# A Mamba block and a ternary FFN on one core: four steps cut into pieces, and every piece placed anew

## The chip, the cores and the metric

One core of a Trainium2 chip. The metric is the device time of one execution in microseconds, the median of several runs; lower is better. Engines: PE (matrix), DVE (vector), ACT (scalar functions and table lookups), POOL (GpSimd), and SP, whose queue issues most of the DMAs.

## The reference

Input x is 2 x 4096 x 256, all float32. Two residual layers follow each other:

```python
x = x + layernorm(mamba(layernorm(x)))      # W_in 1024x256, W_out 256x512
x = x + layernorm(ffn(layernorm(x)))        # hidden 1024, ternary weights

# mamba, per token t, 512 channels e, 16 states s
x_path, z = split(x @ W_in.T); x_path = silu(x_path)
B, C, dt_in, lam_in = split(x_path @ W_x.T)       # 16, 16, 1, 1
B, C = rope(rmsnorm(B + bias)), rope(rmsnorm(C + bias))   # angle: cumulative mean of dt
dt = softplus(dt_in * W_dt + b_dt);  lam = sigmoid(lam_in)
dA = exp(A * dt)
u  = (1 - lam) * dt * dA * Bx_prev + lam * dt * Bx        # Bx = B * x_path
h  = dA * h + u;  y = sum_s(h * C)                        # the scan over t
y  = (y + x_path * D) * silu(z);  out = y @ W_out.T

# ffn
h = gelu(layernorm(x) @ tern(w1).T + b1);  out = layernorm(h) @ tern(w2).T + b2
```

## The kernel before

The sequence is cut into 16 blocks of 512 tokens, 8 for each batch element; the scan state is carried from block to block. A block's scan is cut into 64 units: 4 channel parts j of 128 channels, in each 4 state rounds q of 4 states, in each 4 columns c. A unit is a tile of 128 rows (32 channels x 4 states) by 512 tokens. Four units of one (j, q) make a group and share a tile g.

For one group the work goes round like this:
- `inputs` (L1076): POOL multiplies B by the loaded weighted input `vr` into g, 128 x 2044.
- `decay` (L232): ACT computes exp(A dt) of one unit into a PSUM bank `da`; there are four such banks. `enter` (L1084) writes the carried state into the first column of g.
- `unit_scan`: DVE runs the recurrence. For the first `SPLIT[q]` columns (2, 1, 2, 1 for the four rounds) the result stays in `da` (L1092), and DVE multiplies it by C (`product_v`, L1115, and a copy of the last state, L1116); for the other columns it goes into g (L1095).
- `last` (L1104): ACT copies the last states out of g. `product_g` (L1111): POOL multiplies those columns of g by C in place.
- `sum` (L1127): PE sums the states of the whole g into the bank `y`. Then g is free; there are three g buffers. `start_y` (L1121) has put the skip term `dx` into `y` before, `gate` (L1139) multiplies the finished `y` by silu(z). There is one `y` bank.

Beside the scan of block k run two plans. The plan ahead prepares block k + 1: norm, projections (`project`, `keep`), silu of x, the B/C projection (`bc_project`), softplus of dt (`softplus`), transposes of dt (`dt_turn`, `dt_keep`), the diagonal matrices `mix` and `ddot` (`diag_lam`, `diag_dot`, L912), with which PE weights dt (`weigh`, `skip`, L927), silu of z (`silu_z`), angles, sines and rotations, stores of dt, v and B/C to DRAM and their loads in scan layout (`load_dt`, `load_v`, `load_b`, `load_c`, by SP). `initial` (POOL, `ini`) makes the carried state. The plan behind takes block k - 1 through the output projection, the residual, the norm, the first FFN layer (`ffn_1`, `ffn_keep`), Gelu, the second layer (`ffn_2`, L1202 and L1211, then `ffn_sums`, `ffn_out`), the last norm and the store (`finish`, L1263). Block 0's preparation has a table of places of its own, and in block 0 a plan of 29 steps (`W_AT`) prepares the ternary weights.

The order is written out by hand. A unit has three places; a block has 192. Each step of the plans has a place in `AT` (in `AT_FIRST` for block 0), each step of the scan a distance `LAG` from its unit:

```python
due.setdefault(max(3 * u + lags[i], 0), []).append((what, u))
...
at_place(3 * base)
at_place(3 * base + 1)
if cur is not None:
    unit_scan(cur, j, q, c)
at_place(3 * base + 2)
```

A place is only an order: each engine takes its instructions in the order in which they were issued and waits for what each one needs. Where a tile has no free buffer yet, its instruction stands behind the one that frees it. ACT loads a function table whenever `special` (L230, L232) asks for a function that the loaded table lacks: Exp and Ln share one, Silu and Sin another, Softplus and Gelu have their own.

Of the kernel before, what the change touches and what calls it, by code (L numbers as in the profile page):

```python
# [8 lines left out]
F32 = mybir.dt.float32  # L9
# [5 lines left out]
P = 128  # L15
# [34 lines left out]
    "decay": (-4, -6, -5, -7, 1, -1, 0, 1, -2, -2, -4, -11, 0, -8, -8, -9, 1, 1, -2, -4, -2, -1, -3, -8, -5, -5, -3, -3, 1, -7, -2, -13, -5, -4, -6, -3, -3, -3, -3, -2, -5, -7, 0, -2, -11, -9, -8, -3, -3, -4, -8, -12, -8, -4, -2, -3, -5, -7, -3, -7, -2, 0, -11, -11,),  # L50
    "inputs": (-7, -4, -1, -5, -5, -7, -1, -13, -4, -11, -5, -1, -8, -4, -4, 0,),
    "enter": (-5, -7, -9, -4, -9, -6, -7, -8, -5, -5, -8, -7, -9, -9, -8, -1,),
    "product_v": (8, 20, 4, 4, 7, 4, 4, 4, 5, 9, 4, 4, 11, 4, 4, 4, 11, 10, 4, 4, 4, 4, 4, 4, 7, 4, 4, 4, 4, 4, 4, 4, 23, 6, 4, 4, 5, 4, 4, 4, 5, 2, 4, 4, 5, 4, 4, 4, 3, 11, 4, 4, 2, 4, 4, 4, 5, 4, 4, 4, 11, 4, 4, 4,),
    "last": (21, 12, 11, 11, 12, 15, 14, 14, 19, 12, 11, 8, 16, 12, 20, 11,),
    "product_g": (30, 18, 14, 15, 13, 23, 16, 14, 24, 13, 16, 22, 22, 17, 20, 11,),
    "gate": (26, 31, 37, 25,),
    "start": (24, 17, 19, 27,),
    "sum": (31, 25, 19, 22, 20, 28, 17, 26, 24, 20, 19, 25, 38, 21, 28, 17,),
}

W_AT = (4, 20, 54, 57, 59, 63, 64, 76, 72, 62, 90, 103, 73, 77, 103, 115, 127, 152, 153, 156, 157, 144, 160, 167, 169, 169, 174, 175, 183)
AT = {
    "a_stats": (8, 9,),
    "a_power": (15,),
    "a_offset": (16,),
    "a_apply": (16, 16,),
    "a_turn": (19, 19,),
    "a_evict": (20, 20,),
    "project": (23, 30, 32, 22, 54, 62, 44, 62,),
    "keep": (25, 30, 34, 22, 62, 66, 54, 69,),  # L70
    "silu_x": (36,),
    "bc_project": (45, 48,),
    "bc_take": (61,),
    "dt_project": (75,),
    "bc_square": (98,),
    "bc_power": (112,),
    "dt_row": (75,),
    "dt_spread": (85,),
    "softplus": (89,),
    "bc_scale": (134,),  # L80
    "dt_turn": (103, 112, 110, 109,),
    "dt_keep": (106, 114, 111, 110,),
    "dt_sum": (115,),
    "angles": (125, 126, 127, 129, 130, 130, 132,),
    "diag_lam": (122,),
    "silu_z": (153,),
    "sines": (150,),
    "rotate_a": (155,),
    "rotate_b": (156,),
    "bc_turn": (159,),  # L90
    "bc_store": (163,),
    "dot_sum": (159,),
    "dot_shift": (179,),
    "dot_take": (180,),
    "weigh": (122, 132, 147, 161,),
    "weigh_x": (130, 132, 157, 169,),
    "over": (132,),
    "over_x": (134,),
    "spread": (171,),
    "carry": (177,),  # L100
    "diag_dot": (192,),
    "skip": (206, 201, 198, 195,),
    "skip_x": (208, 205, 206, 197,),
    "initial": (181, 226,),
    "x_next": (190,),
    "load_dt": (137, 217, 246, 278,),
    "load_v": (138, 234, 236, 322,),
    "load_b": (183, 170, 198, 218,),
    "load_c": (185, 186, 192, 212,),
    "x_load": (27,),  # L110
    "out_project": (39, 41,),
    "out_square": (39, 49,),
    "out_power": (39, 52,),
    "residual": (47, 54,),
    "h_stats": (52, 58,),
    "h_power": (61,),
    "h_offset": (63,),
    "h_apply": (68, 63,),
    "h_turn": (68, 71,),
    "h_evict": (74, 76,),  # L120
    "ffn_1": (82, 95, 83, 112, 94, 88, 116, 104,),
    "ffn_keep": (83, 101, 85, 119, 98, 94, 124, 109,),
    "gelu": (128, 129,),
    "ffn_2": (137, 150, 165, 184,),
    "ffn_sums": (144, 158, 175, 196,),
    "ffn_out": (148, 162, 180, 199,),
    "ffn_square": (170, 172, 199, 200,),
    "ffn_power": (172, 206,),
    "ffn_scale": (190, 207,),
    "finish": (207, 209,),  # L130
# [3 lines left out]
    "a_stats": (-181, -241,),  # L134
    "a_power": (-177,),
    "a_offset": (-169,),
    "a_apply": (-160, -134,),
    "a_turn": (-99, -85,),
    "a_evict": (-98, -81,),
    "project": (-79, -79, -79, -79, 4, 5, 1, 5,),  # L140
    "keep": (-79, -79, -79, -79, 7, 11, 6, 15,),
    "silu_x": (-74,),
    "bc_project": (-70, -70,),
    "bc_take": (-79,),
    "dt_project": (-79,),
    "bc_square": (-79,),
    "bc_power": (-46,),
    "dt_row": (-79,),
    "dt_spread": (-79,),
    "softplus": (-79,),  # L150
    "bc_scale": (-43,),
    "dt_sum": (-53,),
    "dt_turn": (-72, -76, -79, -79,),
    "dt_keep": (-54, -56, -79, -75,),
    "angles": (-45, -43, -42, -36, -36, -33, -32,),
    "diag_lam": (-46,),
    "silu_z": (43,),
    "sines": (-32,),
    "rotate_a": (-29,),
    "rotate_b": (-29,),  # L160
    "bc_turn": (-12,),
    "bc_store": (-12,),
    "dot_sum": (-21,),
    "dot_shift": (0,),
    "dot_take": (0,),
    "weigh": (-25, 0, 13, 0,),
    "weigh_x": (-22, 0, 16, 0,),
    "diag_dot": (0,),
    "skip": (0, 0, 0, 0,),
    "skip_x": (0, 0, 1, 1,),  # L170
    "load_dt": (-70, 19, 46, 98,),
    "load_v": (-22, 40, 41, 81,),
    "load_b": (-5, -3, 0, 30,),
    "load_c": (-2, -4, 10, 43,),
    "bc_project_first": (-79, -79, -79, -79,),
    "decay_rates": (-13,),
# [4 lines left out]
def mamba_ffn_kernel(  # L181
# [574 lines left out]
    def softplus(s):  # L756
        if s.k == 0:
            special(freqs, freqs, AF.Softplus)

            nc.vector.tensor_scalar_mul(freqs, freqs, 1.0 / DI)  # L760
        s.dt = p1.tile([P, NJ, T], F32, tag="dt", name=f"dt_{s.k}")
        for j in range(NJ):
            dt = s.dt[:, j, :]
            special(dt, s.pb, AF.Softplus, scale=wdt[:, j : j + 1], bias=bdt[:, j : j + 1])
            nc.sync.dma_start(s.dt_d[j * P : (j + 1) * P, :], dt)
# [142 lines left out]
    def diagonal(s, col, name):  # L908
        t = p1.tile([P, NC4, P + 1], F32, tag="dg", name=f"{name}_{s.k}", bufs=2)
        m = mixed if name == "mix" else ident  # L910
        for c in range(NC4):
            nc.scalar.activation(t[:, c, 0 : m.shape[1]], m, AF.Copy, scale=col[:, c : c + 1])  # L912
        return t

    def diag_lam(s):
        s.mix = diagonal(s, s.lam, "mix")

    def diag_dot(s):
        s.ddot = diagonal(s, s.remdot, "ddot")
# [276 lines left out]
    def ffn_2(s, c, po=None):  # L1196

        if po is None:
            po = ps_ff.tile([P, DM + 1 + P], F32, tag="ff", name=f"pf_{s.k}_{c}")
        for f in range(NH):  # L1200
            gT = s.h1[:, f, c * P : (c + 1) * P]
            nc.tensor.matmul(  # L1202
                po[:, 0 : DM + 1],
                lhsT=gT,
                rhs=w2q[:, f, :],
                start=(f == 0),
                stop=(f == NH - 1),
                skip_group_check=True,
            )

            nc.tensor.matmul(  # L1211
                po[:, DM + 1 :],
                lhsT=gT,
                rhs=gT,
                start=False,
                stop=False,
                skip_group_check=True,
            )
        nc.tensor.matmul(
            po[:, DM + 1 :], lhsT=ident, rhs=deps, start=False, stop=True, skip_group_check=True  # L1220
        )
        s.ff["po", c] = po

    def ffn_sums(s, c):
        k, po = s.k, s.ff["po", c]
        junk = p1.tile([P, DM], F32, tag="junk", name=f"junk2_{k}_{c}")
        ss = small.tile([P, 1], F32, tag="ssf", name=f"ssf_{k}_{c}")
        nc.vector.scalar_tensor_tensor(
            junk[:, 0:P], po[:, DM + 1 :], 1.0 / HID, ident, ALU.mult, ALU.mult, accum_out=ss
        )  # L1230
        m = small.tile([P, 1], F32, tag="mf", name=f"mf_{k}_{c}")
        nc.scalar.activation(m, po[:, DM : DM + 1], AF.Square, scale=1.0 / HID)
        s.ff["rs", c] = small.tile([P, 1], F32, tag="rsf", name=f"rsf_{k}_{c}")
        root(s.ff["rs", c], m, -1.0, ss)
# [54 lines left out]
    def tail(s):  # L1289
# [42 lines left out]
        for c in range(NC4):  # L1332
            ffn_2(s, c, ps_da.tile([P, DM + 1 + P], F32, tag="da", name=f"pf_{k}_{c}"))
        rg = small.tile([P, NC4], F32, tag="rs", name=f"rg_{k}")
        so = small.tile([P, NC4], F32, tag="hsum", name=f"so_{k}")
        for c in range(NC4):
            ffn_sums(s, c)
            ffn_out(s, c)
# [27 lines left out]
    def plan_ahead(s, prev):  # L1366
# [37 lines left out]
        add("softplus", softplus, s)  # L1404
# [7 lines left out]
        add("diag_lam", diag_lam, s)  # L1412
        add("silu_z", silu_z, s, range(NJ))
# [18 lines left out]
        add("diag_dot", diag_dot, s)  # L1432
# [13 lines left out]
    def plan_behind(s):  # L1446
# [32 lines left out]
        for c in range(NC4):  # L1479
            add("ffn_2", ffn_2, s, c, i=c)  # L1480
            add("ffn_sums", ffn_sums, s, c, i=c)
            add("ffn_out", ffn_out, s, c, i=c)
# [148 lines left out]
```

## Time and profile before

| what | us |
|---|---|
| median of three runs | 1990.8 (1989.3 to 1993.0) |
| profiled execution | 1991.1 |
| its span | 1989.4 |
| busy: PE / DVE / ACT / POOL | 1787.7 / 1693.5 / 1658.7 / 1726.1 |
| one I product (L1076, 2044 wide) | 3.81 |
| one P product (L1111, 1024 or 1536 wide) | 2.00 or 2.91 |
| one scan (L1092, L1095) | 1.22, 1.21 |
| one decay (L232, 512 wide) | 0.68 |
| one table load | 1.28 |

The span is the time from the first to the last instruction in the profile. An engine's idle time is given in front of the instruction that ended it, with the engine or DMA that it had waited for. The profile models the ends of matmuls, so PE's busy time is an upper figure.

### The profile page before, as it was taken

How to read it: one execution, taken by the hardware profiler on the slowest of the kernel's cores; microseconds unless marked ns; L12 is line 12 of the kernel's file. 1: busy time of each engine (PE TensorE's matmuls, PEld its weight loads, DVE VectorE, ACT ScalarE, POOL GpSimd, SP SyncE). 2: the span in 40 equal slices, each digit the busy share in tenths (PEclk: the TensorE clock that was granted, in tenths of full speed). 3: DMA queues.
4: the chain of work that ended last, by engine and by line, in shares of the span. 5: the costliest groups of instructions: out<-in, count | busy, mean ns of one | idle time of the engine just before them, and what ended most of it. 6: DMA issues, size and time to landing. Idle time of an engine off the chain costs nothing. (4 is left out here: it accounts for less than half of the span.)

```text
span 1989.4 us, 28676 instructions
## 1 busy us (share of the span) xinstructions
PE 1787.7 (90%) x8938; PEld 1073.7 (54%) x8938; DVE 1693.5 (85%) x2742; ACT 1658.7 (83%) x3832; POOL 1726.1 (87%) x863
## 2 busy tenths in 40 slices
PE   6876998989899998999999898999989999998678
PEld 3434465554646556464655646465564646555257
DVE  1699899988979998898989889799988989898961
ACT  6666988979889897989889798898979898896754
POOL 3689999999989999999989899899999999899960
PEclk7876999999989999999989999899999999898798
DMA  6734545453454645346454534545453464545300
GB/s 118 175 90 111 134 113 138 122 142 89 124 135 114 138 118 146 88 120 152 103 138 122 142 90 123 134 116 138 118 145 89 120 152 103 138 112 139 69 22 11
DMA packets 155721, 233.41 MB, mean 117 GB/s; under 512 B 30160, under 2 KB 55824, under 8 KB 155568
## 3 DMA queue, kind: packets, MB, share of 16 engines
q1 hardware_dynamic: 153440, 230.80, 47.5%
q0 software_dynamic: 544, 0.71, 0.3%
q8 instruction: 70, 1.15, 0.3%
q14 instruction: 83, 0.68, 0.1%
q10 hardware_dynamic: 1584, 0.07, 0.1%
HBM read 188.51 MB, written 42.99 MB: 116 GB/s over the span
## 5 line engine op out<-in xcount | busy, mean ns | idle before, releaser
L1076 POOL TENSOR_TENSOR g<-b,vr 128x2044 f32<-128x2044 f32 (+1 forms) x256 | 975.2, 3812 | 113.3 <-PE y L1127 81.2
L1095 DVE TENSOR_TENSOR_SCAN g<-da,g 128x512 f32<-128x512 f32 x640 | 753.3, 1207 | 17.2 <-ACT da L232 12.0
L232 ACT ACTIVATE da<-dtr,aneg 128x512 f32<-128x512 f32 x1024 | 682.1, 683 | 64.4 <-DVE g L1095 47.2
L1111 POOL TENSOR_TENSOR g<-c,g 128x1024 f32<-128x1024 f32 (+1 forms) x256 | 626.4, 2456 | 47.7 <-ACT hl L1104 26.5
L1092 DVE TENSOR_TENSOR_SCAN da<-da,g 128x512 f32<-128x512 f32 x384 | 462.2, 1221 | 118.9 <-POOL g L1076 86.6
L1127 PE MATMUL y<-g,fold 128*32 128x512 f32 x2048 | 324.6, 650 | 44.9 <-POOL g L1111 28.9
L1202 PE MATMUL pf<-w2q,h 128*128 128x257 f32 x1024 | 312.8, 387 | 16.2 <-DVE o L1239 13.1
L651 PE MATMUL pz<-oT_a,wi 128*128 128x512 f32 x512 | 277.1, 685 | 2.0 <-ACT oT_a L603 0.7
L1180 PE MATMUL ph<-oT_h,w1q 128*128 128x512 f32 x480 | 238.2, 620 | 32.8 <-ACT h L1190 10.0
L1115 DVE TENSOR_TENSOR g<-da,c 128x512 f32<-128x512 f32 x384 | 257.3, 675 | 5.6 <-DMA c<-bc_d 3.4
L1211 PEld LDWEIGHTS pf<-h 128*128 128x128 f32 x1024 | 195.3, 191 | 27.6
L1211 PE MATMUL pf<-h 128*128 128x128 f32 x1024 | 197.2, 274 | 0.0
L651 PEld LDWEIGHTS pz<-oT_a,wi 128*128 128x128 f32 x512 | 104.7, 219 | 153.6 <-issue 101.5
L1202 PEld LDWEIGHTS pf<-w2q,h 128*128 128x128 f32 x1024 | 156.0, 192 | 33.3 <-ACT g L1084 19.8
L1180 PEld LDWEIGHTS ph<-oT_h,w1q 128*128 128x128 f32 x480 | 82.4, 191 | 153.2 <-issue 59.9
L1127 PEld LDWEIGHTS y<-g,fold 128*32 128x32 f32 x2048 | 50.0, 111 | 194.0 <-issue 60.9
L230 ACT ACT_TABLE_LOAD x97 | 124.5, 1283 | 1.7
L927 PE MATMUL pw<-ddot,dtT 128*128 128x128 f32 (+1 forms) x512 | 77.6, 296 | 49.3 <-DVE dx L1007 22.9
L1149 PE MATMUL po<-wo,zs 128*128 128x256 f32 x480 | 107.6, 382 | 0.0
L927 PEld LDWEIGHTS pw<-ddot,dtT 128*128 128x128 f32 x512 | 65.8, 193 | 69.8 <-ACT ddot L912 30.8
L1149 PEld LDWEIGHTS po<-wo,zs 128*128 128x128 f32 x480 | 90.0, 190 | 24.2 <-ACT hl L1104 11.7
L927 PEld LDWEIGHTS ps<-mix,dtT 128*128 128x128 f32 x512 | 69.4, 196 | 32.6 <-issue 30.9
(238 smaller groups left out, 2421.4 us busy)
## 6 DMA issues: line engine op xcount, KB each, us to landing
dtr<-dt_d SPq DMA_DIRECT2D x256, 256.0 KB, 5.1
vr<-v_d SPq DMA_DIRECT2D x256, 256.0 KB, 6.6
dt_d<-dt SPq DMA_DIRECT2D x64, 256.0 KB, 5.4
v_d<-v SPq DMA_DIRECT2D x64, 256.0 KB, 2.0
b<-bc_d SPq DMA_DIRECT2D x256, 64.0 KB, 2.2
c<-bc_d SPq DMA_DIRECT2D x256, 64.0 KB, 2.1
xpre<-in_L_attn_x_dram SPq DMA_DIRECT2D x16, 512.0 KB, 3.8
xpost<-in_L_attn_x_dram SPq DMA_DIRECT2D x15, 512.0 KB, 6.1
```

What stands on the lines that cost most here:

```text
L232: nc.scalar.activation(dst, src, f, **kw)
L651: nc.tensor.matmul(s.pz[e], lhsT=wi[:, kk, e * P : (e + 1) * P], rhs=s.na.oT[:, kk, :], start=(kk == 0), stop=(kk == 1),)
L927: nc.tensor.matmul(ps[:, c * P - 1 + skip : c * P - 1 + n], lhsT=s.dtT[c][:, j * P : (j + 1) * P], rhs=diag[:, c, skip:], start=start and ...
L1076: nc.gpsimd.tensor_mul(states(s, j, q)[:, :, t0:], s.bcq[0, q][:, None, t0:].to_broadcast([P, NG, T - t0]), s.ch[j, "vr"][:, :, t0:],)
L1092: nc.vector.tensor_tensor_scan(da, da, g, 0.0, ALU.mult, ALU.add)
L1095: nc.vector.tensor_tensor_scan(g, da, g, 0.0, ALU.mult, ALU.add)
L1111: nc.gpsimd.tensor_mul(g, s.bcq[1, q][:, None, :].to_broadcast([P, NG - n, T]), g)
L1115: nc.vector.tensor_mul(s.g[j, q][:, c, :], da, s.bcq[1, q])
L1127: nc.tensor.matmul(s.ys[j][c * G : (c + 1) * G, :], lhsT=fold, rhs=g[:, c, :], start=False, stop=(q == NQ - 1), skip_group_check=True,)
L1180: nc.tensor.matmul(s.ph[f], lhsT=w1q[:, kk, f * P : (f + 1) * P], rhs=s.nh.oT[:, kk, :], start=(kk == 0), stop=(kk == 1),)
L1202: nc.tensor.matmul(po[:, 0 : DM + 1], lhsT=gT, rhs=w2q[:, f, :], start=(f == 0), stop=(f == NH - 1), skip_group_check=True,)
L1211: nc.tensor.matmul(po[:, DM + 1 :], lhsT=gT, rhs=gT, start=False, stop=False, skip_group_check=True,)
```

## The change

Four steps are cut into more pieces, each with a place of its own: `softplus` of one block from one step into four (one for each 128 channels, with its DMA), `silu_z` from one into four, `diag_lam` and `diag_dot` from one into four each (one for each 128 tokens), and `ffn_2` of each 128 tokens from one into four (two of the eight hidden tiles each). `ffn_sums` is cut in two: the sums, and the root (`ffn_root`). All tables of places (`LAG`, `W_AT`, `AT`, `AT_FIRST`) get new numbers. No instruction on PE, DVE, POOL or SP is added or dropped.

```diff
 LAG = {
-    "inputs": (-7, -4, -1, -5, -5, -7, -1, -13, -4, -11, -5, -1, -8, -4, -4, 0,),
-    "product_g": (30, 18, 14, 15, 13, 23, 16, 14, 24, 13, 16, 22, 22, 17, 20, 11,),
-    "gate": (26, 31, 37, 25,),
-    "start": (24, 17, 19, 27,),
-    "sum": (31, 25, 19, 22, 20, 28, 17, 26, 24, 20, 19, 25, 38, 21, 28, 17,),
+    "inputs": (-6, 1, 0, -5, -11, -4, -8, -4, -2, -5, -1, -8, -14, -3, -3, -6,),
+    "product_g": (21, 18, 18, 14, 22, 26, 15, 24, 19, 15, 16, 17, 26, 15, 23, 24,),
+    "gate": (28, 37, 25, 35,),
+    "start": (26, 17, 25, 28,),
+    "sum": (28, 24, 19, 16, 22, 26, 21, 30, 29, 28, 22, 20, 39, 17, 37, 31,),
...
-W_AT = (4, 20, 54, 57, 59, 63, 64, 76, 72, 62, 90, 103, 73, 77, 103, 115, 127, 152, 153, 156, 157, 144, 160, 167, 169, 169, 174, 175, 183)
+W_AT = (2, 24, 36, 40, 41, 49, 61, 78, 76, 66, 81, 84, 112, 123, 129, 130, 136, 144, 147, 154, 159, 142, 161, 161, 163, 164, 173, 185, 195)
 AT = {
-    "softplus": (89,),
-    "diag_lam": (122,),
-    "silu_z": (153,),
-    "sines": (150,),
-    "diag_dot": (192,),
-    "load_v": (138, 234, 236, 322,),
-    "ffn_2": (137, 150, 165, 184,),
+    "softplus": (89, 95, 95, 90,),
+    "diag_lam": (119, 119, 124, 106,),
+    "silu_z": (145, 144, 146, 145,),
+    "sines": (143,),
+    "diag_dot": (175, 178, 188, 186,),
+    "load_v": (157, 214, 240, 245,),
+    "ffn_2": (136, 136, 136, 137, 144, 147, 148, 155, 164, 168, 169, 171, 183, 186, 188, 188,),
+    "ffn_root": (142, 162, 176, 197,),
...
 AT_FIRST = {
-    "bc_power": (-46,),
-    "softplus": (-79,),
-    "silu_z": (43,),
-    "load_c": (-2, -4, 10, 43,),
+    "bc_power": (-69,),
+    "softplus": (-65, -63, -62, -68,),
+    "silu_z": (63, 40, 62, 54,),
+    "load_c": (-2, -2, 16, 9,),
...
-    def softplus(s):
-        if s.k == 0:
+    def softplus(s, j):
+        if s.k == 0 and j == 0:
             special(freqs, freqs, AF.Softplus)
             nc.vector.tensor_scalar_mul(freqs, freqs, 1.0 / DI)
-        s.dt = p1.tile([P, NJ, T], F32, tag="dt", name=f"dt_{s.k}")
-        for j in range(NJ):
-            dt = s.dt[:, j, :]
-            special(dt, s.pb, AF.Softplus, scale=wdt[:, j : j + 1], bias=bdt[:, j : j + 1])
-            nc.sync.dma_start(s.dt_d[j * P : (j + 1) * P, :], dt)
+        s.own("dt", lambda: p1.tile([P, NJ, T], F32, tag="dt", name=f"dt_{s.k}"))
+        dt = s.dt[:, j, :]
+        special(dt, s.pb, AF.Softplus, scale=wdt[:, j : j + 1], bias=bdt[:, j : j + 1])
+        nc.sync.dma_start(s.dt_d[j * P : (j + 1) * P, :], dt)
...
-    def diagonal(s, col, name):
-        t = p1.tile([P, NC4, P + 1], F32, tag="dg", name=f"{name}_{s.k}", bufs=2)
+    def diagonal(s, col, name, c):
+        t = s.own(
+            name, lambda: p1.tile([P, NC4, P + 1], F32, tag="dg", name=f"{name}_{s.k}", bufs=2)
+        )
         m = mixed if name == "mix" else ident
-        for c in range(NC4):
-            nc.scalar.activation(t[:, c, 0 : m.shape[1]], m, AF.Copy, scale=col[:, c : c + 1])
-        return t
+        nc.scalar.activation(t[:, c, 0 : m.shape[1]], m, AF.Copy, scale=col[:, c : c + 1])
...
-    def ffn_2(s, c, po=None):
+    def ffn_2(s, c, fs=range(NH), po=None):
         if po is None:
-            po = ps_ff.tile([P, DM + 1 + P], F32, tag="ff", name=f"pf_{s.k}_{c}")
-        for f in range(NH):
+            if ("po", c) not in s.ff:
+                s.ff["po", c] = ps_ff.tile([P, DM + 1 + P], F32, tag="ff", name=f"pf_{s.k}_{c}")
+            po = s.ff["po", c]
+        for f in fs:
...
+    def ffn_root(s, c):
+        m, ss = s.ff.pop(("sums", c))
+        s.ff["rs", c] = small.tile([P, 1], F32, tag="rsf", name=f"rsf_{s.k}_{c}")
         root(s.ff["rs", c], m, -1.0, ss)
...
-        add("softplus", softplus, s)
+        for j in range(NJ):
+            add("softplus", softplus, s, j, i=j)
...
-        add("silu_z", silu_z, s, range(NJ))
+        for j in range(NJ):
+            add("silu_z", silu_z, s, (j,), i=j)
...
         for c in range(NC4):
-            add("ffn_2", ffn_2, s, c, i=c)
+            for i in range(4):
+                add("ffn_2", ffn_2, s, c, range(2 * i, 2 * i + 2), i=4 * c + i)
             add("ffn_sums", ffn_sums, s, c, i=c)
+            add("ffn_root", ffn_root, s, c, i=c)
```

## The prediction

> **What bounds the kernel now.** I read the page's busy times first, then stretches of the middle, the waits of blocks 1 to 14, and POOL's rows in order.
>
> ```profile
> span 1989.4 us, 28676 instructions
> ...
> PE 1787.7 (90%) x8938; PEld 1073.7 (54%) x8938; DVE 1693.5 (85%) x2742; ACT 1658.7 (83%) x3832; POOL 1726.1 (87%) x863
> ```
>
> Four engines within 7 points of each other: no engine has much room. One stretch of the middle (engines in the order PE, PEld, DVE, ACT, POOL) says it for the steady state:
>
> ```profile
> 425.00:544.00 119.00, 109.20 (x566) 66.40 (x566) 107.30 (x174) 103.16 (x241) 109.48 (x57) 0.97 0.49 123
> ```
>
> POOL, PE and DVE are busy for 90 to 92%. POOL's wide `ini` addition comes once a block, first at 212.54 us and, 14 blocks on, at 1835.62 us: a block takes (1835.62 - 212.54)/14 = 115.9 us. The start and the end are 212.5 and 153.8 us. What is to be had in a block is the idle time between the busy pieces. Who waits, between 188 and 1833 us (total, times, longest):
>
> ```profile
> POOL g L1076 <- PE y L1127: 67.6, 60, 2.6
> DVE da L1092 <- POOL g L1076: 65.6, 35, 2.1
> ...
> ACT da L232 <- DVE g L1095: 37.7, 43, 4.4
> ```
>
> This is a ring. POOL's input product (L1076, called I below) fills one of three g buffers, DVE scans it, POOL's output product (L1111, P) multiplies it in place, PE sums it (L1127), and only then is the buffer free for the third I after it. I name the groups by channel part and state round: I31 is j=3, q=1. POOL's rows of one block show where the ring closes too late (start, length, then idle before it and who ended it):
>
> ```profile
> 1148.34 3.81 POOL L1076 TENSOR_TENSOR g<-b,vr 128x2044 f32<-128x2044 f32 x1
> 1152.86 2.00 POOL L1111 TENSOR_TENSOR g<-c,g 128x1024 f32<-128x1024 f32 x1 [0.71 <-ACT hl L1104]
> 1154.82 0.20 POOL L578 TENSOR_TENSOR nm_h<-nm_h,rs_h 128x4 f32<-128x4 f32 x1
> 1156.08 3.81 POOL L1076 TENSOR_TENSOR g<-b,vr 128x2044 f32<-128x2044 f32 x1 [1.06 <-PE y L1127]
> 1160.70 3.81 POOL L1076 TENSOR_TENSOR g<-b,vr 128x2044 f32<-128x2044 f32 x1 [0.81 <-POOL g L1076]
> ...
> 1198.25 2.00 POOL L1111 TENSOR_TENSOR g<-c,g 128x1024 f32<-128x1024 f32 x1
> 1201.51 3.81 POOL L1076 TENSOR_TENSOR g<-b,vr 128x2044 f32<-128x2044 f32 x1 [1.26 <-PE y L1127]
> ...
> 1220.21 3.81 POOL L1076 TENSOR_TENSOR g<-b,vr 128x2044 f32<-128x2044 f32 x1 [1.47 <-PE y L1127]
> ...
> 1247.49 2.90 POOL L1111 TENSOR_TENSOR g<-c,g 128x1536 f32<-128x1536 f32 x1 [1.66 <-issue]
> 1251.24 3.81 POOL L1076 TENSOR_TENSOR g<-b,vr 128x2044 f32<-128x2044 f32 x1 [0.85 <-PE y L1127]
> ```
>
> In turn: I11, P10, I12, I13; P22 with I31 right behind it (nothing on POOL hides the sum, so the whole latency of 1.26 us shows); I33; P01 and I03 of the next block. Over the eleven blocks that can be read row by row, POOL's mean idle is P10 0.68, I12 1.11, I13 0.59, P12 0.31, rem 0.33, I22 0.40, I31 1.26, I33 1.47, P00 0.47, P01 1.30, I03 0.86: 8.8 us a block.
>
> **What the change does to the work: nearly nothing.** The orders of both programs hold as many instructions on PE, DVE, POOL and SP; ACT has 3 more, all table loads (133 against 130). The pieces hardly come apart: softplus's four stay together but for one small copy, silu of z's four are adjacent in a steady block, three of the four `ffn_2` calls still run unbroken on PE, the fourth has one sum in its middle. Only the diagonals spread. So what is new is the order.
>
> **The order on POOL, position by position.** Before: `P03 I11 P10 nm I12 I13 P11 P12`; after: `P03 I11 I12 nm P10 I13 P11 P12`.
> - P10: I12's 3.8 us now lie ahead of it, so the scan and copy it waited for are done: 0.68 to 0.
> - I12: the same sum is needed, but PE now has half the B/C projection (`pbc` in two runs of 8) ahead of that sum instead of all of it, and I11's 3.8 us cover it: 1.11 to 0.
> - I13: P10 now stands directly before it, and I13 needs P10's sum. The row of that shape is I31's: 0.59 to 1.26.
> - I22: `P13 I22` becomes `P13 P20 I22`, 2.0 us of cover: 0.40 to 0.1 (between 0 and 0.40).
> - I31: `P22 I31` becomes `P22 P23`, three rotations, `I31`: 2.9 + 1.1 us cover the 1.26: to 0.
> - I33 still follows P31 directly: 1.47 stays. P12 and rem stay, 0.31 and 0.33.
> - P00: before, P00 came after I02 while DVE held the first group up. DVE's work from the block's first scan to the end of group 00, by the rows (scans 1.22 and 1.21, dx 0.74, o 0.47, junk 0.36 with its read-out, product and copy 0.82, norm statistics 2.1), was 2 x 1.22 + 2 x 1.21 + 0.36 + 0.74 + 0.47 + 0.82 + 2.1 = 9.35 us; now dx, product and statistics stand behind it: 5.7 us. To 0.
> - P01: group 01 ends 1.5 us earlier by the same sum (a gate of 0.68 and a product of 0.82 go behind it), and ACT's copy `hl`, once queued behind an eviction that waits for PE, now has only oT and one decay ahead: 1.30 to 0.6 (0 to 1.30).
> - I03: gate and `start_y` move behind group 01, and the one y bank is free later, so the sum of 00 is no earlier though P01 and I02 cover more: 0.86 stays (0 to 0.86).
>
> Left: 1.26 + 0.31 + 0.33 + 0.1 + 1.47 + 0.6 + 0.86 = 4.9 us, 3.9 us a block less on POOL. Over 15 blocks (14 periods and the last, which has the same ring) 58 us if nothing else became late. But DVE is busy 107.3 and PE 109.2 of 119 us, POOL 109.5: with POOL's period 3.9 us shorter PE would stand at 95%. The bounds are 0 and 58 us; I take half, 29, since PE, DVE and ACT have no more than 9.8, 11.7 and 15.8 us of that stretch free, and each queue is ordered anew.
>
> **The start.** Today ACT works `ms` (Ln, Exp) off between the transposes of dt and the sines, with a table load of its own: 1.28 + 0.30 + 0.21 us from 35.48 us on, on the way to the first B/C store. After, `ms` follows the Exp of lam, which has that table, and waits for DVE's reduction; dt starts some 0.3 us later, and the load is gone: -1.5 us. The c load of round 3 goes from behind `vr` of parts 1 and 2 on SP to ahead of them; DVE waited 3.35 us and POOL 2.26 us for c near 85 to 91 us. I take -2 us (0 to -5.6): the next load, b of round 3, still stands behind the weight load, and POOL waited 5.42 us for it.
>
> **Table loads in block 0.** Silu of z in block 0 is cut into three groups between decays: four switches more, less the one saved.
>
> ```profile
> 906.36 1.31 ACT L232 ACTIVATE da<-dtr,aneg 128x512 f32<-128x512 f32 x2
> 907.68 1.28 ACT L230 ACT_TABLE_LOAD   x1
> 908.98 1.91 ACT L232 ACTIVATE xp<-xp 128x2048 f32<-128x2048 f32 x1
> ```
>
> From the end of the decay (907.67) to the next instruction a switch takes 1.31 us. Four are 5.2 us, between 60 and 120 us, where the page's stretch view has ACT busy 39.5 of 60 us: they are covered at 0 by ACT's 20 idle us, and cost up to 5.2 if a scan waits for the decay behind them. The Trainium skill's page "ScalarE: Activation LUTs" (What ACT_TABLE_LOAD costs) speaks against such cuts and sets a switch at 1.28 us plus a drain of 1.38, 2.66 in all; by it the four would be an estimated 10.6 us. No drain shows in these rows, so the sum keeps 1.31.
>
> **Queues passed.** SP has the same DMAs; `vr` of part 0 now waits behind v of parts 1 and 2, but 29 places (17 us) before its use. The load of x for block 2 comes after the weights (place 195 instead of 183) with 9 places, 5.4 us, to its statistics; loads of x land in 3.8 us (page), so 0 to 2 us, taken as 0. The tail is untouched.
>
> **The sum.** Profiled execution 1991.1 us (span 1989.4, 1.7 around it; the median of the runs, 1990.8, is 0.3 lower): 1991.1 - 29 - 1.5 - 2 = 1958.6, so 1958 us as a median.
>
> **Rivals.**
> - *The freed waits come back elsewhere.* For: PE at 92%, its waits on ACT evictions, the ring's 65.6 us of DVE waiting for POOL. Then only the start's 3.5 us remain, less up to 5.2 of table loads: 1987.6 to 1992.8, about 1988, range 1978 to 1998. It contains the case that pieces left adjacent do nothing.
> - *DVE starves: slower.* I02, I22 and I31 each go behind one more P (2.0, 2.0 and 2.9 us), so their scans may start up to 6.9 us a block later. Place: `DVE da <- POOL g`, already 4.7 us a block. It decides when DVE's own work between the scan that the P waits for and the group's first scan is shorter than P plus I: 2.0 + 3.8 = 5.8 us for I02 and I22, 7.9 us for I31. By the rows one group's four scans, products and copies are 4 x 1.21 + 1.5 x 0.82 = 6.1 us, plus side work: thin cover. With half of the 6.9 uncovered against 1.9 saved, +1.5 us x 15 = 23 us on 1987.6: 2011; all uncovered, +5.0 x 15, 2063. Range 1998 to 2045. Against: DVE has gate, v and o2 work in just these places.
>
> **Chances.** Forecast 0.52 (1925 to 1980), given back 0.24 (0.09 faster, 0.09 the same, 0.06 slower), starving 0.24. The same means within 0.2%, 4 us, which is what a measurement of this kernel can tell. Faster 0.52 + 0.09 = 0.61, same 0.09, slower 0.06 + 0.24 = 0.30. Low end 1920: all 58 us and the start's 7 reach 1926, with some room. High end 2015 takes in half of the starving case; left out are some 0.04 below and 0.12 above.
>
> **What would show it.** Right: POOL's idle per block near 6 to 7 us, no idle before I31 and P10, about 1.3 us before I13, a period of 114 us, `POOL g <- PE y` well under 67.6. Given back: those waits gone at a period of 116, with PE or ACT rows in their place. Starving: `DVE da <- POOL g` far above 65.6 us, before the first scans of 02, 22 and 31. The forecast is wrong if the period is above 115.

## The result, and the profile after

| | before | after |
|---|---|---|
| median, 15 runs each (us) | 1991.6 (1989.3 to 1994.2) | 1997.4 (1988.7 to 2006.0) |
| profiled execution, span (us) | 1991.1, 1989.4 | 1999.8, 1998.1 |
| first I of block 0, of block 2 (us) | 53.5, 297.9 | 57.6, 303.1 |
| period: from the first I of block 2 to that of block 15, over 13 (us) | 116.08 | 116.37 |

The change is slower by 0.3%: ratio 1.0031 [1.0018, 1.0045]. The forecast was 1958, faster; the direction was wrong. The runs of after also spread more than three times as far (17.3 against 4.9 us).

The page's busy times and the same stretch of the middle, both of after:

```profile
span 1998.1 us, 28791 instructions
...
PE 1787.2 (89%) x8938; PEld 1083.5 (54%) x8938; DVE 1690.8 (85%) x2742; ACT 1660.6 (83%) x3835; POOL 1726.9 (86%) x863
```
```profile
425.00:544.00 119.00, 110.92 (x563) 67.88 (x561) 106.36 (x176) 103.87 (x244) 108.62 (x54) 0.94 0.50 121
```

The work is the same to the instruction but for three table loads on ACT. POOL does 0.9 us less of it in those 119 us than before, so what was to be gained on POOL is not there. The waits of blocks 1 to 14 (188 to 1833 us; total, times, longest), from the answers for POOL, DVE and ACT, say where it went:

```profile
POOL rem L747 <- DVE lam L742: 33.2, 13, 4.0
POOL g L1076 <- PE y L1127: 26.8, 35, 1.3
...
DVE da L1092 <- ACT da L233: 80.1, 20, 6.9
...
ACT da L233 <- DMA dtr<-dt_d: 29.3, 13, 3.6
```

The same wait of DVE in the kernel before:

```profile
DVE da L1092 <- ACT da L232: 13.8, 20, 2.0
```

POOL's wait for PE's sums went from 67.6 to 26.8 us, as forecast, and DVE's for POOL, 65.6 us before, has left the head of the list (1.7). In their place DVE waits 80.1 us for ACT's decay (13.8 before), and that decay for the load of `dtr`. POOL's rows of one block of after (start, length, idle before them):

```profile
1155.18 2.91 POOL L1111 TENSOR_TENSOR g<-c,g 128x1536 f32<-128x1536 f32 x1 [1.24 <-DMA vr<-v_d]
1158.05 7.58 POOL L1076 TENSOR_TENSOR g<-b,vr 128x2044 f32<-128x2044 f32 x2
1165.58 0.20 POOL L579 TENSOR_TENSOR nm_h<-nm_h,rs_h 128x4 f32<-128x4 f32 x1
1165.74 2.00 POOL L1111 TENSOR_TENSOR g<-c,g 128x1024 f32<-128x1024 f32 x1
1169.00 3.81 POOL L1076 TENSOR_TENSOR g<-b,vr 128x2044 f32<-128x2044 f32 x1 [1.26 <-PE y L1127]
...
1188.74 0.22 POOL L747 TENSOR_SCALAR rem<-lam 128x4 f32<-128x4 f32 x1 [2.55 <-DVE lam L742]
```

These are P03, I11 with I12 right behind it, the norm step, P10, I13 and, in the next part, `rem`. P10 and I12 have no idle left and I13 has 1.26 us, to the hundredth what the prediction said. `rem`, which was to keep 0.33, waits 2.55 us: DVE is late for it. One block later the whole chain can be read in four views, SP's queue, POOL, ACT and DVE (last number in SP's rows: DMAs in that row; 26.71 us is two loads of `vr` with the wait between them):

```profile
1263.42 26.71 SPq L1030 DMA_DIRECT2D vr<-v_d  x8
1290.22 1.80 SPq L1030 DMA_DIRECT2D dtr<-dt_d  x4
```
```profile
1284.55 3.81 POOL L1076 TENSOR_TENSOR g<-b,vr 128x2044 f32<-128x2044 f32 x1 [1.26 <-PE y L1127]
```
```profile
1300.17 0.69 ACT L233 ACTIVATE da<-dtr,aneg 128x512 f32<-128x512 f32 x1 [1.90 <-DMA dtr<-dt_d]
```
```profile
1300.96 2.35 DVE L1092 TENSOR_TENSOR_SCAN da<-da,g 128x512 f32<-128x512 f32 x2 [5.31 <-ACT da L233]
```

There are two `vr` buffers. The load of `vr` of part 3 can only go when I13, the last reader of part 1, is done: 1284.55 + 3.81 = 1288.36. The load of `dtr` of part 2 needs nothing that is late, but stands behind it on SP and goes at 1290.22. The decay of part 2 gets its data at 1300.17, after 1.90 us of waiting for them, and DVE has stood for 5.31 us. Not all of the 5.31 is the load's: 3.28 us of it stay in e1 below, where the decay waits for no load but stands behind softplus on ACT. While SP stood, the DMA engines had nothing to do, from 1275 to 1289 us in this view (DMA share in 40 slices of 1275 to 1305 us, 0.75 us each; 0 is under 10%):

```profile
DMA  0000000000000000000899999999999999999999
```

Of the kernel before the same place reads as follows. The first row holds `dtr` of part 2, issued at once at 1256.91, and `dtr` of part 3, issued at 1285.61 after a wait of 26.5 us for ACT; `vr` of part 3 goes last, after the stores of dt, and waits for nothing.

```profile
1256.91 30.43 SPq L1030 DMA_DIRECT2D dtr<-dt_d  x8
1287.70 2.33 SPq L765 DMA_DIRECT2D dt_d<-dt  x4
1290.12 2.66 SPq L1030 DMA_DIRECT2D vr<-v_d  x4
```

The Trainium skill's page "Perfetto Trace Analysis" (DMA Instruction — HWDGE) says that the sequencer waits for a DMA's semaphores first and is free for its next instruction only when the DMA has been issued. The rows above agree: nothing was issued between the two loads of `vr`, and `dtr` 0.1 us after the second.

### The profile page after: what moved, and what is told of

It reads as the page before. It is cut to its first block, busy times and chain, and to the rows that moved or that the text cites. A ratio compares the mean times of both kernels' runs of the same rounds, so it can differ in the third digit from the quotient of the medians.

```text
span 1998.1 us, 28791 instructions
## 1 busy us (share of the span) xinstructions
PE 1787.2 (89%) x8938; PEld 1083.5 (54%) x8938; DVE 1690.8 (85%) x2742; ACT 1660.6 (83%) x3835; POOL 1726.9 (86%) x863
## 4 chain that ended last, share of the span: by engine, by line
PE 34%; ACT 26%; DMA 16%; DVE 12%; issue 4%; POOL 3%; SPq 3%; ACTq 0%; DVEq 0%; POOLq 0%
ACT da L233 10%; PE pf L1204 10%; DMA dtr<-dt_d 8%; PE pf L1213 5%; DVE g L1095 4%; PE y L1127 4%; DMA vr<-v_d 4%; DVE da L1092 4%; PE ph L1180 3%; DMA c<-bc_d 3%; SPq L1030 2%; PE pz L652 2%; POOL g L1076 2%; PE ps L939 2%; PE pw L927 2%
## 5 line engine op out<-in xcount | busy, mean ns | idle before, releaser
L1095 DVE TENSOR_TENSOR_SCAN g<-da,g 128x512 f32<-128x512 f32 x640 | 757.5, 1210 | 32.3 <-ACT da L233 26.5
L1092 DVE TENSOR_TENSOR_SCAN da<-da,g 128x512 f32<-128x512 f32 x384 | 462.3, 1220 | 119.9 <-ACT da L233 90.9
L1127 PE MATMUL y<-g,fold 128*32 128x512 f32 x2048 | 327.9, 645 | 29.8 <-POOL g L1111 17.3
L1204 PE MATMUL pf<-w2q,h 128*128 128x257 f32 x1024 | 317.7, 392 | 11.4 <-DVE v L951 5.6
L652 PE MATMUL pz<-oT_a,wi 128*128 128x512 f32 x512 | 248.9, 620 | 10.6 <-ACT oT_a L604 5.4
L1180 PE MATMUL ph<-oT_h,w1q 128*128 128x512 f32 x480 | 250.4, 656 | 8.3 <-ACT h L1190 5.8
L652 PEld LDWEIGHTS pz<-oT_a,wi 128*128 128x128 f32 x512 | 91.2, 193 | 145.5 <-issue 86.2
L1180 PEld LDWEIGHTS ph<-oT_h,w1q 128*128 128x128 f32 x480 | 91.4, 208 | 126.9 <-issue 83.7
L927 PE MATMUL pw<-ddot,dtT 128*128 128x128 f32 (+1 forms) x512 | 91.8, 336 | 44.3 <-DVE dx L1007 41.2
L927 PEld LDWEIGHTS pw<-ddot,dtT 128*128 128x128 f32 x512 | 79.8, 237 | 61.9 <-DVE dx L1007 55.7
L789 PE MATMUL pdtT<-ident,dt 128*128 128x128 f32 x256 | 49.1, 325 | 51.8 <-ACT h L1190 47.8
```

The source lines that it names most:

```text
L652: nc.tensor.matmul(s.pz[e], lhsT=wi[:, kk, e * P : (e + 1) * P], rhs=s.na.oT[:, kk, :], start=(kk == 0), stop=(kk == 1),)
L927: nc.tensor.matmul(ps[:, c * P - 1 + skip : c * P - 1 + n], lhsT=s.dtT[c][:, j * P : (j + 1) * P], rhs=diag[:, c, skip:], start=start and ...
L1092: nc.vector.tensor_tensor_scan(da, da, g, 0.0, ALU.mult, ALU.add)
L1095: nc.vector.tensor_tensor_scan(g, da, g, 0.0, ALU.mult, ALU.add)
L1127: nc.tensor.matmul(s.ys[j][c * G : (c + 1) * G, :], lhsT=fold, rhs=g[:, c, :], start=False, stop=(q == NQ - 1), skip_group_check=True,)
L1180: nc.tensor.matmul(s.ph[f], lhsT=w1q[:, kk, f * P : (f + 1) * P], rhs=s.nh.oT[:, kk, :], start=(kk == 0), stop=(kk == 1),)
```

## The experiments

The theory that the traces suggest (A in the expectations): the new order on POOL earns about what was forecast, and the blocked SP queue eats it up. Its rivals: the order on POOL earns nothing, or DVE's starving or the cut pieces are what costs. Every ratio is against runs of the kernel before beside it on the same chip (medians 1988.9 to 1993.6). The period is that of the first table.

| kernel | us | ratio to before | period | first I of block 2 |
|---|---|---|---|---|
| e1: after, `vr` of part 3 behind `dtr` of part 2 | 1946.4 | 0.9776 [0.9757, 0.9795] | 113.18 | 296.8 |
| e13: after, `dtr` of part 2 ahead of `vr` of part 3 | 1954.2 | 0.9803 [0.9778, 0.9828] | 113.15 | 303.3 |
| e2: before, `vr` of part 3 ahead | 2043.2 | 1.0266 [1.0239, 1.0293] | 118.87 | 304.2 |
| e4: e1 with POOL's old order at three places | 2001.2 | 1.0043 [1.0028, 1.0058] | 116.70 | 303.6 |
| e5: before with POOL's new order there | 2096.0 | 1.0528 [1.0509, 1.0547] | 123.04 | 311.6 |
| e9: e5 with one copy `hl` earlier | 2018.2 | 1.0134 [1.0111, 1.0157] | 117.95 | 300.8 |
| e3: e1 with the pieces joined outside block 0 | 1958.7 | 0.9831 [0.9813, 0.9850] | 113.19 | 303.8 |
| e10: e1 with `ffn_2` joined | 1955.1 | 0.9819 [0.9796, 0.9841] | 113.20 | 302.3 |
| e7: e1 with silu of z of block 0 joined | 1949.6 | 0.9786 [0.9770, 0.9803] | 113.15 | 302.1 |
| e6: e1 with two decays ahead of softplus | 1988.4 | 0.9974 [0.9961, 0.9987] | 115.73 | 306.3 |
| e11: e1 with one decay ahead | 1954.3 | 0.9819 [0.9796, 0.9842] | 113.43 | 301.2 |
| e12: e1 with one sum on PE earlier | 1947.3 | 0.9785 [0.9765, 0.9806] | 112.88 | 300.6 |

### The order of two loads on SP: e1, e13, e2

```diff
-    "load_v": (157, 214, 240, 245,),   # after, to e1
+    "load_v": (157, 214, 240, 259,),
-    "load_dt": (141, 223, 258, 311,),  # after, to e13
+    "load_dt": (141, 223, 244, 311,),
-    "load_v": (138, 234, 236, 322,),   # before, to e2
+    "load_v": (138, 234, 236, 245,),
```

> The changed kernel with one number altered: the load of vr for channel part 3 stands behind the load of dtr for part 2 on SP's queue (place 259 instead of 245). Theory A (blocked queue): in the changed kernel the vr load waits on SP for the third g product of part 1, and the dtr load behind it comes so late that DVE idles 5.2 to 6.9 us before the first scan of part 2 in nearly every block (90.9 us in all). With the order turned, these waits go, the wait of the decay on the dtr load (38.1 us) too, and the period falls from 116.3 to between 111 and 114 us: 1920 to 1965 us. Rival B (no room elsewhere): PE, DVE and ACT are near full, the 5.5 us come back as other waits, and the time stays within 0.5% of the changed kernel, 1987 to 2007 us.

> This is the kernel after with the load of dtr of part 2 issued at place 244 instead of 258, so one place ahead of vr of part 3, which stays at 245; e1 got the same order of the two by moving vr of part 3 behind. If the order of the two on SP is what costs the change its gain, e1's time comes back: 1943 to 1956 us, with periods of 113.0 to 113.7 us and no wait of over 4 us of DVE before the first scan of part 2. If the place of vr of part 3 counts for itself (its transfer beside other work, or the loads of b and c behind it), most of the loss stays: 1975 to 2000 us.

> The kernel before with one number altered: the load of vr for part 3 is put ahead of the load of dtr for part 2 (place 245 instead of 322), as the changed kernel has it. Theory A: the blocked queue costs by itself: DVE waits for the first decay of part 2 by some 3 to 6 us a block, 1991 + 15 x 3 to 6 = 2035 to 2080 us. Rival B: the load is early enough in this order, or the wait falls into idle time that is there already: below 2005 us.

One number of after's tables gives 51 us back, and e1 beats both kernels by over 2%. e13 changes the other load's place and gets 43 us back and the same period to 0.02 us, so it is the order of the two that counts, not where `vr` of part 3 lands. (The 8 us between e1 and e13 lie ahead of block 2 and behind block 15.) SP's queue and DVE in e1, the block that answers to the one above, and DVE's wait over the whole span:

```profile
1234.29 3.41 SPq L1030 DMA_DIRECT2D dtr<-dt_d  x4
1257.19 1.73 SPq L1030 DMA_DIRECT2D vr<-v_d  x4
```
```profile
1267.74 2.35 DVE L1092 TENSOR_TENSOR_SCAN da<-da,g 128x512 f32<-128x512 f32 x2 [3.28 <-ACT da L233]
```
```profile
DVE da L1092 <- ACT da L233: 47.7, 16, 3.3
```

`dtr` is now issued 22.9 us ahead of `vr` of part 3 instead of behind it. SP still waits for POOL before its loads of `vr`, 28 times in both kernels (those of parts 2 and 3, nearly all of it part 3), 389.0 us in after and 337.6 in e1 over the whole span; only the follower has changed. DVE's wait for the decay falls from 90.9 us (whole span) to 47.7. In the mean of blocks 2 to 14 DVE stands 5.50 us before the first scan of part 2 in after and 3.28 in e1, and 1.1 us before groups 21 and 22 in after and nothing in e1: together the 3.2 us by which the periods differ.

The same step in the kernel before, e2, costs 2.7%, some 50 us. DVE's wait at this place grows from 2.02 to 4.76 us a block, by as much as the period (2.78). The profile puts it down to "issue" or to POOL there, but the decay of that scan ends just ahead of it and had waited for `dtr`, as in after (ACT, then DVE):

```profile
1323.73 0.69 ACT L232 ACTIVATE da<-dtr,aneg 128x512 f32<-128x512 f32 x1 [2.06 <-DMA dtr<-dt_d]
```
```profile
1324.63 2.34 DVE L1092 TENSOR_TENSOR_SCAN da<-da,g 128x512 f32<-128x512 f32 x2 [4.10 <-issue]
```

### The order on POOL: e4, e5, e9

```diff
-    "inputs": (..., -8, ..., -1, ..., -3, ...),       # I12, I22, I31: e1, to e4
+    "inputs": (..., -1, ..., -5, ..., -4, ...),
-    "product_g": (..., 22, ..., 19, ..., 17, ...),    # P10, P20, P23
+    "product_g": (..., 13, ..., 24, ..., 22, ...),
-    "sum": (..., 20, ...),                            # of group 23, behind P23
+    "sum": (..., 23, ...),
```

e5 has the reverse in the kernel before, with the sum of group 10 two places later (20 to 22), behind its P10. e9 is e5 with one number more:

```diff
-    "last": (21, 12, 11, 11, 12, 15, 14, 14, 19, ...),   # hl of group 20
+    "last": (21, 12, 11, 11, 12, 15, 14, 14, 13, ...),
```

> This is e1 with POOL's order of the kernel before at three places: P10 ahead of I12, I22 ahead of P20, I31 ahead of P23 (the sum of group 23 follows its product). If POOL's order is what makes e1 faster than the kernel before, the terms of the prediction come back: P10 0.68 + I12 1.11 + I22 0.3 + I31 1.26 less I13 0.67 = 2.7 us a block, 40 us over 15 blocks, of which at least half: 1966 to 1986 us, with idle of about 1.2 us on POOL before I31 and about 1 us before I12. If the order at these places is worth nothing (its waits come back elsewhere, and e1's gain lies in the other queues), 1942 to 1951 us.

> This is the kernel before with POOL's order of the change at the same three places and nothing else. If POOL's order earns by itself, half to all of 2.7 us a block: 1951 to 1972 us. If it earns only with the rest of the change's order on DVE, PE and ACT, 1985 to 1997 us. If the later I of 12, 22 and 31 starves DVE (the rival of the prediction, 5.8 to 7.9 us of cover), over 2000 us, with DVE's waits for POOL above 86.6 us.

> This is e5 (the kernel before with POOL's new order at three places) with ACT's copy hl of group 20 six places earlier (lag 13 instead of 19, as in the change). In e5 P20 waits 3.9 us for that copy, and I22, now behind P20, makes DVE wait 4.6 us. If the copy is what the new POOL order lacked, about 3.5 to 4.5 us a block come back, 2096 less 50 to 65: 2030 to 2045 us, with no wait of over 1 us before P20. If DVE simply lacks cover for P plus I, the wait for ACT turns into one for DVE and the time stays at 2080 to 2096 us.

e4: with the old order at three places 55 us are lost again, 3.5 us a block, above the 40 that the terms sum to. POOL's idle time before its I, P, `rem` and `nm_h` is 9.8 us a block in e4 and 6.3 in e1, so it differs by as much as the period. Its rows show the idle times that the forecast had taken away, in one place under another name: where the prediction counted I12's wait, `nm_h` waits for ACT, with I12 behind it instead of ahead to cover it (P10, `nm_h`, I22, I31):

```profile
1163.36 1.99 POOL L1111 TENSOR_TENSOR g<-c,g 128x1024 f32<-128x1024 f32 x1 [0.72 <-DVE g L1095]
1167.20 0.20 POOL L579 TENSOR_TENSOR nm_h<-nm_h,rs_h 128x4 f32<-128x4 f32 x1 [1.84 <-ACT rs_h L233]
...
1193.73 3.81 POOL L1076 TENSOR_TENSOR g<-b,vr 128x2044 f32<-128x2044 f32 x1 [1.55 <-PE y L1127]
...
1214.29 3.81 POOL L1076 TENSOR_TENSOR g<-b,vr 128x2044 f32<-128x2044 f32 x1 [1.54 <-issue]
```

e5: the same order put into the kernel before costs 104 us, as the third expectation had it; DVE's waits for POOL are 181.1 us over the whole span. POOL at P20 and I22, and DVE at the first scan of group 22:

```profile
1246.89 2.00 POOL L1111 TENSOR_TENSOR g<-c,g 128x1024 f32<-128x1024 f32 x1 [3.91 <-ACT hl L1104]
1248.85 3.81 POOL L1076 TENSOR_TENSOR g<-b,vr 128x2044 f32<-128x2044 f32 x1
```
```profile
1252.70 2.35 DVE L1092 TENSOR_TENSOR_SCAN da<-da,g 128x512 f32<-128x512 f32 x2 [4.58 <-POOL g L1076]
```

P20 waits 3.91 us for ACT's small copy `hl` of group 20, which the old order had put late because P20 came late. I22 now stands behind P20, so DVE waits 4.58 us for it. In e9 that one copy is issued six places earlier, and POOL's row has no idle:

```profile
1196.68 2.00 POOL L1111 TENSOR_TENSOR g<-c,g 128x1024 f32<-128x1024 f32 x1
```

This gives 78 us back, 5.1 a block, more than the 50 to 65 expected. e9 is still 1.3% slower than the kernel before: DVE's waits for POOL stay at 120.3 us over the whole span, against 86.6 before and 19.5 in e1. Of this growth only 0.64 us a block stands before group 22, the rival's place (DVE starved by an I behind one more P), and nothing before 12 and 31; the rest stands where DVE waited already (03, 20 and 33), before group 20 for as long as before. The largest wait that is new, 1.0 us a block before group 13, is for a decay on ACT. So the rival is real where the rest of the order is the old one, but small. Which of the other new places take the remaining waits away was not taken apart.

### The pieces: e3, e10, e7

```diff
-    "softplus": (89, 95, 95, 90,),        # e1, to e3
-    "diag_lam": (119, 119, 124, 106,),
-    "silu_z": (145, 144, 146, 145,),
-    "diag_dot": (175, 178, 188, 186,),
+    "softplus": (90, 90, 90, 90,),
+    "diag_lam": (119, 119, 119, 119,),
+    "silu_z": (145, 145, 145, 145,),
+    "diag_dot": (186, 186, 186, 186,),
-    "ffn_2": (136, 136, 136, 137, 144, 147, 148, 155, 164, 168, 169, 171, 183, 186, 188, 188,),  # e1, to e3 and e10
+    "ffn_2": (137, 137, 137, 137, 155, 155, 155, 155, 171, 171, 171, 171, 188, 188, 188, 188,),
-    "silu_z": (63, 40, 62, 54,),          # AT_FIRST: e1, to e7
+    "silu_z": (43, 43, 43, 43,),
```

> The same as the kernel with vr of part 3 behind dtr of part 2, but the pieces of softplus, silu of z, both diagonals and the second FFN layer are joined again outside block 0: all pieces of one step get one place (softplus 90, silu of z 145, diagonals 119 and 186, the four FFN calls 137, 155, 171 and 188). Theory A: the pieces stood together anyway and only the order of scan, products, sums and loads matters: within 0.4% of the kernel with the pieces apart. Rival: cutting is what gives room, above all the one sum that gets into the middle of an FFN call and the diagonals between decays: 0.5 to 2% slower than with the pieces apart.

> This is e1 with the four pieces of each ffn_2 call joined again outside nothing else: softplus, silu of z and the diagonals stay in pieces. With all pieces joined (e3) the time was 1958.7, 12 us over e1. If the layer's pieces are what counted there (DVE waited 8 us more for PE's pf), 1952 to 1960 us. If it was the spread diagonals or silu of z, 1944 to 1949 us.

> This is e1 with silu of z of block 0 in one run (place 43) instead of three groups between decays: four table switches of 1.31 us less. If they are covered, as the prediction took it, 1943 to 1949 us, with the start of block 1 unmoved within 2 us of e1's. If they lie on the path, 5.2 us less: 1940 to 1942 us. If one run of four silus holds decays up longer than the switches did, up to 6 us more: 1949 to 1953 us.

The pieces joined again leave the period where it was: 113.19 against 113.18. By its time e3 falls into the rival's range (0.6% slower than e1), by its period it does not: e3 and e10 are 12 and 9 us slower than e1, but those microseconds lie ahead of block 2 and behind block 15, and e13, with the pieces as in after, has its first I of block 2 as late (303.3). What the pieces earn by themselves is thus nothing in a steady block and 0.6% at most in all; whether it is more than nothing stays open. e7: four table switches less in block 0 gain nothing (1949.6 against 1946.4, intervals that overlap). Its number lies in the third range of its expectation, but its first I of block 0 already comes 3.3 us later than e1's, ahead of any silu of z; from there to the first I of block 1 it takes 133.0 us, e13 with the switches 132.8. So they are covered, as the prediction took them, as far as such runs can tell.

### Idle time that is left: e6, e11, e12

In e1 DVE still idles 3.3 us a block ahead of part 2's first scan, whose decay stands behind softplus and two table loads. e6 moves two decays ahead of them, e11 one. e12 takes I33's wait of 1.3 to 1.5 us for a sum that PE does late.

```diff
-    "decay": (..., 0, -2, ...),      # units 0 and 1 of group 20: e1, to e6
+    "decay": (..., -8, -11, ...),
-    "decay": (..., 0, ...),          # unit 0 alone: e1, to e11
+    "decay": (..., -8, ...),
-    "sum": (..., 39, ...),           # of group 30; "start" of part 3 from 28 to 27: e1, to e12
+    "sum": (..., 29, ...),
```

> This is e1 with the first two decays of part 2 moved ahead of softplus on ACT. In e1 DVE idles 3.3 us in most blocks before the first scan of part 2, which waits for the decay that stands behind softplus and its two table loads. If that idle lies on the path, 1.5 to 3.3 us a block go: 1900 to 1925 us. If something takes its place (dt comes 1.2 us later to PE's transposes, the third decay is still behind softplus), 1935 to 1955 us and the same idle in another row.

> This is e1 with only the first decay of part 2 ahead of softplus, where e6 moved two and took 1988 us. If the price of e6 is that decays made early hold the four PSUM buffers that FFN1 shares, one of them costs about half: 1960 to 1972 us. If softplus being 0.6 us later for each is what costs, 1955 to 1975 us also, with PE's transposes of dt later by 0.6 us. If one decay is enough cover for the first scan and holds nothing up, 1.2 us a block are gained: 1925 to 1940 us.

> This is e1 with the sum of group 30 ten places earlier on PE, and the copy that starts y of part 3 one place earlier. In e1 PE does this sum behind two pieces of ffn_2 and so I33 on POOL waits 1.3 to 1.5 us a block. If POOL's remaining idle lies on the path as the prediction's POOL terms did, 1.3 us a block or half of it: 1926 to 1938 us, with no idle before I33. If PE stalls on the sum until P30 is done and its other work falls behind, 1948 to 1965 us, with PE waits for POOL in its place.

None gains measurably. DVE's waits over the whole span, first of e11, then of e6:

```profile
DVE da L1092 <- POOL g L1076: 50.9, 24, 5.8
...
DVE da L1092 <- ACT da L233: 20.9, 16, 1.4
```
```profile
DVE g L1095 <- ACT da L233: 52.2, 47, 2.2
DVE da L1092 <- POOL g L1076: 51.4, 26, 5.2
```

e11 takes 26.8 us from DVE's wait for ACT (47.7 to 20.9) and gets 31.4 more of the wait for POOL (19.5 to 50.9): behind the decay was the input product of the same group, for which DVE waits 2.2 us a block where it waited 3.3 for the decay, and the second decay, now behind softplus, adds 1.4. In e6 the third decay, now behind softplus, adds 27 us to a third wait (25.2 to 52.2), and the period grows by 2.6 us; DVE's waits at this group explain 0.8 us of that, the rest was not taken apart. The step from one decay to two costs 34 us; the first costs 0.3 us a block, and the other half of its 8 us lies ahead of block 2. The split by half that was expected is wrong. e12's period is 0.3 us shorter, 4 us over the blocks, and its block 2 begins 3.9 us later than e1's; I33 still has 1.08 us of its wait. No kernel here is measurably faster than e1.

## Why the prediction was wrong

- **Queues passed: the step that failed.** It said "SP has the same DMAs" and followed `vr` of part 0 and the load of x. It did not compare the order of all loads: `load_v` of part 3 goes from 322 to 245, which puts it ahead of `load_dt` of part 2 (246 before, 258 after), and it is the one load there that must wait for a buffer. The term, taken at 0, is 3.2 us a block (116.37 - 113.18); turning the order of the two loads gave 51 us in e1 and 43 in e13. No rival named it either: "given back" (1988) came nearest in size, but looked for the waits on PE and ACT evictions.
- **The order on POOL: right.** Without the blocked queue the period falls by 2.9 us (116.08 to 113.18); the bound was 3.9 and half of it was taken, a choice between the bounds and no working-out. e1's 1946 lies below the 1958 forecast. POOL's idle time before its I, P, `rem` and `nm_h`, in the mean of blocks 2 to 14, is 9.0 us a block before, 9.5 after and 6.3 in e1; 6 to 7 was the sign of being right. Position by position, in after: P10, I12, I31 and P00 to 0, I22 to 0.1 and I13 to 1.26, as said. P01, put at 0.6, I03, put at 0.86, and P12, put at 0.31, have none, I33 at 1.47 has 1.27. Not foreseen were P03 (0.85 us), I10 and I20 (0.4 each) and P20 to P23 (0.4 to 0.7 each); `rem`, 2.57 in after, is back at 0.35 in e1. On DVE the gain stands before groups 03 and 33: 1.88 us each before, at most 0.04 in after and e1.
- **DVE starves: did not happen in after** (its waits for POOL fell from 86.6 to 16.0 us over the whole span). e5 and e9 show that the mechanism is real in the old order: 4.55 and 0.64 us a block before group 22, the difference being a late copy on ACT, which the prediction's sum of DVE's cover did not hold. Before 02 and 31, its other places, DVE waits no more than 0.03 us in either.
- **The start: wrong by its sign.** -3.5 us was forecast, -1.5 of it ahead of the first I, which comes 4.1 us later. 0.8 us of this is the change's: PE's first projections start at 13.36 instead of 12.59, because the second half of their input is now evicted ahead of the first, which they read first. 2.1 us more is the time of these projections (10.12 against 7.97 us), which the last section takes up and which varies with the run. From the first B/C projection to the first I it is 34.26 us against 33.05: the table load of `ms` is gone, but the sines then wait 1.65 us for DVE's angles. Over the profiled executions of the ten kernels with the new start this stretch took 33.9 us in the mean, of the four with the old one 33.6, and the first I comes at 56.5 and 54.8 us. So some 1.6 of the 4.1 us are the change's as far as 14 profiles tell, and the -1.5 shows nowhere. The -2 for `c` stays open: its waits near 85 to 91 us are gone, and from the first I of block 0 to that of block 1 it is 130.3 us in after against 132.3 before, but 131.6 in e1 and 132.8 in e13, which have the same block 0.
- **Table loads in block 0: right**, at 0, as far as e7 can tell.
- **What would show it:** the period above 115 showed the forecast wrong, as it was to; the row that told why, `DVE da <- ACT da`, was on no list.

## What to carry to other kernels

When a change moves DMA issues, write out the order of every load on the queue, and for each the instruction that frees its buffer: a load whose buffer comes free late belongs behind all those that could go at once. An order on one engine is bought together with its partners: the new order on POOL is worth 55 us with the rest of the order that was placed for it and costs 104 without, 78 of them through one small copy on ACT. The longest wait in the list is not the gain: e11 took 27 us of it away and gained nothing.

## What the runs showed of the hardware that was not expected

PE's first projections, the same 16 matmuls, took 7.97 us in the profiled execution of before and 10.12 in that of after:

```profile
12.59 7.97 PE L651 MATMUL pz<-oT_a,wi 128*128 128x512 f32 x16
L651 PE MATMUL pz<-oT_a,wi x2: 951/1087/1223, 12.6 to 13.6; 128*128 128x512 f32 x2
```
```profile
13.36 10.12 PE L652 MATMUL pz<-oT_a,wi 128*128 128x512 f32 x16 [0.68 <-ACT oT_a L604]
L652 PE MATMUL pz<-oT_a,wi x7: 974/1057/1219, 13.4 to 18.6; 128*128 128x512 f32 x7
```

The second row of each gives the matmuls that start before 14.3 us (before) and 19.4 us (after), with the least, median and greatest time in ns: two in before, seven in after. From then on one takes 0.59 us. The traces say what happens at these moments: their lists of granted clocks begin there, with full clock, at 14.32 us in before and 19.40 in after. (The profile's view of 12 to 24 us gives a granted clock of 1.00 for both, but only because the lists have no entry for the time ahead.) Later in before, matmuls of this form take 1.06 us in the median at a granted clock of 0.5 (65 of them) and 0.59 at 1.0 (416). So by their times the first ones ran at half clock, and five more of them at it make the 2.15 us. In the ten profiles whose projections start at 13.2 to 13.5 us full clock comes between 16.2 and 19.4 us, so it is not the change that sets the moment; what does, the runs do not show.
